# Graph-attention stack on one Trainium2 core: which operand is loaded and which is moved in the attention-times-values product of layers 0 and 1

## The chip, the core and the metric

The kernel runs on one core of one Trainium2 chip. The core has a matrix engine (PE, with its weight load shown apart as PEld), a vector engine (DVE), a scalar engine (ACT), a general engine (POOL, which here issues the gathers) and SyncE (SP, which issues the plain transfers); each takes its instructions in its own order and waits on semaphores of the others. The metric is the device time of one execution in microseconds (us). Three timed runs of the kernel before gave 2251.62, 2253.98 and 2256.02 us, median 2253.98 us.

## What is computed

Four graph-attention layers over 4096 nodes with 256 features, each followed by a residual sum and a layer norm. The adjacency matrix is 4096 x 4096 with about one entry in 256 set, and the diagonal. Layer 0, cut to what matters:

```
h = (x @ W.T)                       # 4 heads of 64
e[h,i,j] = leaky_relu(alpha_src[h,i] + alpha_dst[h,j], 0.2)
attn = softmax over j of e, only where adj[i,j] is set
out[i,h] = sum_j attn[h,i,j] * h[j,h]
x = layernorm(x + out)
```

Layer 1 has the same form with 4 heads of 64, layer 2 has 2 heads of 128, and layer 3 has one head of 256 with a positive and a negative attention, a product and an elu. The change touches the product attn x h of layers 0 and 1.

## The kernel before

**Tiling.** The 4096 nodes are 32 row tiles of 128 (`m`). A program at the start of the kernel (`lists`) finds, for each row tile, the nodes that any of its 128 rows has as a neighbour, and packs them into 13 groups of 128 nodes (`NG`), with the tile's own nodes as a fourteenth (`NP` = 14 positions). For a row tile the attention is then a sum over 14 blocks of 128 x 128 in place of 32. The 14 positions are worked in two halves of 7 (`HALF`).

**One row tile in layers 0 and 1.** `RowTile.load` fetches the scores of the 128 rows (`S`), the packed mask, and for each position 128 rows of values by an indirect gather that POOL issues (line 647; 13 of them, the fourteenth is a plain transfer). A gathered block `G[k]` holds, for each of 4 heads, 65 columns: 64 values already multiplied by the exponential of their score, and that exponential itself, whose weighted sum is the softmax's denominator (`C4` = 65). `RowTile.half` makes the weights `w[h]`, 128 neighbours x 128 rows for each position: heads 0 to 2 by ACT (line 712), head 3 by DVE (lines 704 and 708), and then a maximum and the mask by DVE for two heads at once (line 681: one instruction for heads 3 and 0, one for heads 1 and 2). Then the products: for head 3, 0, 1, 2 in turn and for each of the 7 positions, one fp32 matmul (line 724) in which the 65 value columns are loaded as the stationary operand and the 128 columns of weights move past them. The result, 65 x 128 for each head, is transposed to what is wanted; four heads side by side fill one PSUM bank of 512 columns (`accs[0]`), over both halves. `copy` (line 749, ACT) takes the 65 x 512 out of the bank into `aT`, `back` (line 757, PE) transposes it by heads into another bank, taken from `ptwo[1]`, as 128 x 260, and `finish` (lines 1114 to 1117, DVE) divides by the sums and adds the residual.

Each fp32 matmul shows in the trace as two pairs of a weight load and a matmul, so the 4 x 14 products of a row tile are 112 PE instructions and as many loads.

**Order.** `Layer.half_alone` writes the order of one half step: transposes of a row tile of the following layer, the half of tile m, then the store, the projection, the copy and back of tile m-1 (in part 0) or its finish (in part 1). So tile m-1's copy and back stand behind tile m's first half, and its finish behind the second. The bank `accs[0]` comes from a pool of two (`ptwo[0]`), so tile m+2 takes the bank of tile m. The order of instructions on each engine is laid out when the program is built, from this order, from what is ready and from estimated durations; the lists' work, the projections of the following layer and the attention are interleaved by it. Gathered blocks lie in 16 slots of two positions (`g0`), and from layer 1 on in 14 more (`g1`).

Layer 2 adds whole rows (`whole_rows`, lines 1016 to 1027): for three groups of four row tiles all 32 blocks are worked without packing, and these units fill in between the row tiles.

## Time and profile before

| | |
|---|---|
| median of three timed runs | 2253.98 us |
| span of the profiled execution | 2249.3 us |
| median less span | 4.7 us |
| mean granted PE clock | 0.966 of full speed |
| PE busy, share of the span | 2014.0 us, 90% |
| DVE busy | 1786.6 us, 79% |
| ACT busy | 1737.9 us, 77% |
| POOL busy | 1494.4 us, 66% |
| matmuls of line 724 (layers 0 and 1) | 7168, from 168.7 to 1339.1 us |
| copy of the accumulator, line 749 | 64, 0.57 us each |

The profiled execution's time outside its span isn't recorded on its own; its span is the time that the steps are summed against, and the runs' median lies 4.7 us above it. Read the table with care: busy shares are means over stages. The kernel passes through stages with different limits: building the lists with layer 0 (to about 646 us), the rest of layer 0 (to about 830), layer 1 (to about 1340), layer 2 with its whole rows (to about 1760) and layer 3. A group's idle column says how long the engine stood still before the group's instructions, and who released it; POOL's instructions have a fixed pause between them that is put down as "issue" or to whatever happened last.

### The profile page before, as it was taken

The numbers are of one execution on the slowest core, as the hardware profiler recorded it, in microseconds if no ns is written. First come the engines' busy times: TensorE is split into PE (matmuls) and PEld (weight loads), VectorE is DVE, ScalarE is ACT, GpSimd is POOL, SyncE is SP. The second block draws the span as 40 slices with busy tenths as digits, with TensorE's granted clock in tenths as the row PEclk, the third lists the DMA queues.
The fourth block names the chain that finished last, engine by engine and source line by source line (L and its number), as shares of the span: only waits on it lengthen the run. The fifth ranks groups of instructions, "written<-read, shape, count | busy, mean of one in ns | idle before, by whom it ended". The sixth has DMA issues, their size and how long they took to land. (4 is left out here: it accounts for less than half of the span.)

```text
span 2249.3 us, 49137 instructions
## 1 busy us (share of the span) xinstructions
PE 2014.0 (90%) x15689; PEld 1834.3 (82%) x15689; DVE 1786.6 (79%) x5060; ACT 1737.9 (77%) x4989; POOL 1494.4 (66%) x1597
## 2 busy tenths in 40 slices
PE   4878889989999969988899898989999999999995
PEld 2658788878899859988888798989998888788784
DVE  2889899999999959987988886887876566566566
ACT  4778988988789859987888776987876677667664
POOL 2107655656677777777777777777773477777773
PEclk7999999999999989999999999999999999999998
DMA  8879877777566665666665666777777688888884
GB/s 284 258 245 360 272 219 250 254 247 228 146 170 191 174 202 168 182 175 175 173 185 162 172 167 171 226 209 223 223 227 225 200 282 280 249 284 270 262 248 130
DMA packets 250319, 492.99 MB, mean 219 GB/s; under 512 B 44385, under 2 KB 156610, under 8 KB 249666
## 3 DMA queue, kind: packets, MB, share of 16 engines
q0 software_dynamic: 81536, 245.30, 38.3%
q1 hardware_dynamic: 163906, 240.26, 33.3%
q10 hardware_dynamic: 4608, 4.20, 0.5%
q8 instruction: 126, 2.06, 0.4%
q14 instruction: 143, 1.17, 0.2%
HBM read 437.05 MB, written 52.54 MB: 218 GB/s over the span
## 5 line engine op out<-in xcount | busy, mean ns | idle before, releaser
L647 POOL DMA_INDIRECT G<-vals,idx x1456 | 1480.7, 1017 | 715.7 <-issue 221.1
L712 ACT ACTIVATE w<-S,G 128x128 f32<-128x128 f32 x3248 | 1001.6, 390 | 140.6 <-DMA G<-vals,idx 101.6
L724 PE MATMUL bank<-w,G 128*65 128x128 f32 x7168 | 837.8, 276 | 59.7 <-DVE w L681 59.3
L724 PEld LDWEIGHTS bank<-w,G 128*65 128x65 f32 x7168 | 798.7, 140 | 69.9 <-DVE w L681 68.4
L681 DVE SCALAR_TENSOR_TENSOR w<-w,bank 128x1792 f32<-128x1792 f32 x256 | 514.6, 2013 | 13.4 <-ACT w L712 11.2
L727 PE MATMUL bank<-G,w 128*128 128x257 f32 (+1 forms) x2660 | 490.8, 342 | 25.7 <-ACT z L1102 13.6
L727 PEld LDWEIGHTS bank<-G,w 128*128 128x128 f32 x2660 | 431.9, 195 | 73.2 <-ACT z L1102 16.4
L1027 PE MATMUL bank<-vw,pw 128*128 128x129 f32 (+1 forms) x2048 | 298.5, 301 | 3.7 <-issue 2.3
L1027 PEld LDWEIGHTS bank<-vw,pw 128*128 128x128 f32 x2048 | 273.6, 191 | 20.1 <-issue 2.8
L690 ACT ACTIVATE w<-S,G 128x128 f32<-128x128 f32 x385 | 137.8, 393 | 136.8 <-DMA G<-vals,idx 90.0
L440 DVE TENSOR_SCALAR oh<-iota,place 128x256 bf16<-128x256 f16 (+2 forms) x992 | 221.8, 298 | 9.4 <-PE bank L446 9.1
L704 DVE TENSOR_TENSOR w<-S,G 128x256 f32<-128x256 f32 x384 | 151.9, 416 | 69.9 <-DMA G<-vals,idx 66.5
L446 PE MATMUL bank<-mk,oh 128*128 128x132 fp8e4 x2336 | 192.1, 226 | 13.8 <-ACT cm L453 7.0
L557 PE MATMUL bank<-wext,xT 128*128 128x268 f32 (+3 forms) x640 | 176.9, 409 | 16.9 <-ACT xT L548 14.1
L446 PEld LDWEIGHTS <-oh 128*128 128x128 bf16 x2336 | 146.9, 99 | 50.4 <-DVE oh L440 12.7
L385 ACT ACTIVATE mk<-raw 128x1024 uint8<-128x1024 int32 x128 | 130.5, 1051 | 28.0 <-DMA raw<-in_adjB_dram 27.7
L557 PEld LDWEIGHTS bank<-wext,xT 128*128 128x128 f32 x640 | 117.2, 200 | 36.0 <-ACT xT L548 16.9
L1017 DVE SCALAR_TENSOR_TENSOR pw<-pw,mw 128x512 f32<-128x512 f32 x192 | 127.6, 689 | 18.2 <-ACT pw L1016 17.5
L1016 ACT ACTIVATE pw<-Sw,d 128x512 f32<-128x512 f32 x192 | 133.2, 711 | 7.5 <-PE bank L1027 7.0
L714 DVE SCALAR_TENSOR_TENSOR w<-w,mk 128x896 f32<-128x896 f32 x80 | 86.6, 1086 | 41.1 <-ACT w L712 37.9
L1024 DVE TENSOR_TENSOR pw<-pw,mw 128x512 f32<-128x512 f32 x64 | 43.6, 691 | 85.4 <-ACT pw L1023 48.0
L692 DVE TENSOR_TENSOR w<-w,mk 128x896 f32<-128x896 f32 x55 | 60.0, 1091 | 59.5 <-ACT w L691 58.2
(140 smaller groups left out, 1563.3 us busy)
## 6 DMA issues: line engine op xcount, KB each, us to landing
raw<-in_adjB_dram SPq DMA_DIRECT2D x128, 512.0 KB
mk<-maskC SPq DMA_DIRECT2D x112, 231.0 KB
G<-vals,idx POOLq DMA_INDIRECT x1456
S<-edge SPq DMA_DIRECT2D x64, 256.0 KB
vw<-vals SPq DMA_DIRECT2D x96, 129.0 KB
xp<-y SPq DMA_DIRECT2D x96, 128.0 KB
y<-xp SPq DMA_DIRECT2D x96, 128.0 KB
mw<-maskW SPq DMA_DIRECT2D x20, 528.0 KB
```

Source lines behind the costliest of these rows:

```text
L440: nc.vector.tensor_scalar(oh[:, :n * P], iota[:, :n * P], self.place[:, it, j:j + 1], None, op0=ALU.is_equal)
L446: nc.tensor.matmul(accs[b][:, s * MC:(s + 1) * MC], oh[:, (k - a) * P:(k - a + 1) * P], mk[:, j, it, :].bitcast(FP8), start=touches[b][0] ...
L557: nc.tensor.matmul(pp[:, :c1 - c0], self.xT[:, k, :], wext[:, k, c0:c1], start=(k == 0), stop=(k == KT - 1 and brow is None))
L647: nc.gpsimd.indirect_dma_start(out=self.place(pos), out_offset=None, in_=sh["v"][n][:NODES[t], :], in_offset=bass.IndirectOffsetOnAxis(ap= ...
L681: nc.vector.scalar_tensor_tensor(pair, pair, LEAST, mh2, op0=ALU.max, op1=ALU.mult)
L690: nc.scalar.activation(w[0][:, k, :], S[:, 0, :], AF.Relu, bias=d(k, 0))
L704: nc.vector.tensor_tensor(w[h][:, k:k + 2, :], S[:, h:h + 1, :].to_broadcast([P, 2, P]), dd[:, :, V + T + h:V + T + h + 1].to_broadcast([P ...
L712: nc.scalar.activation(w[h][:, k, :], S[:, h, :], AF.Exp, bias=d(k, h))
L724: nc.tensor.matmul(accs[0][:Wd, h * P:(h + 1) * P], v, w[h][:, k, :], **how)
L727: nc.tensor.matmul(a, w[h][:, k, :], v, **how)
L1016: nc.scalar.activation(p, S[:, h], AF.Exp, bias=d)
L1027: nc.tensor.matmul(accs[it][:, c:c + Wd], p[:, it, :], v[:, c:c + Wd], start=(j == 0 and h == heads[0]), stop=(j == NT - 1), skip_group_ch ...
```

## The change

For heads 3 and 2 the roles are swapped: the weights (128 columns) are loaded and the 65 value columns move past them, so that the result is 128 rows x 65 columns, as wanted. Heads 0 and 1 stay as they were. The products of heads 3 and 0 alternate, position by position, then those of heads 2 and 1. The direct results stand in columns 256 to 385 of the bank, the transposed ones in columns 0 to 255. `copy` takes out 65 x 256 in place of 65 x 512, `back` transposes two heads in place of four, into columns 126 to 255 of the same bank, and `finish` reads columns 126 to 385 of it. No bank of `ptwo[1]` is taken for `back` any more, and `accs[0]` is held until `finish` has read it, where before it came free with `copy`. Layers 2 and 3 keep their products.

```diff
+TWOS = ((3, 0), (2, 1))
...
-            heads = list(range(A, H)) + list(range(A))
+            heads = range(H)
+        if n < 2:
+            for up, flat in TWOS:
+                for k in range(HALF):
+                    pos = half * HALF + k
+                    how = dict(stop=pos == NP - 1, skip_group_check=True)
+                    c = 2 * P + (up - 2) * Wd
+                    nc.tensor.matmul(accs[0][:, c:c + Wd], w[up][:, k, :], G[k][:, up * Wd:(up + 1) * Wd],
+                                     start=pos == 0 and up == TWOS[0][0], **how)
+                    nc.tensor.matmul(accs[0][:Wd, flat * P:(flat + 1) * P], G[k][:, flat * Wd:(flat + 1) * Wd],
+                                     w[flat][:, k, :], start=False, **how)
+            return
         for h in heads:
...
-                if n < 2:
-                    nc.tensor.matmul(accs[0][:Wd, h * P:(h + 1) * P], v, w[h][:, k, :], **how)
-                else:
-                    a = accs[h][:, :Wd] if n == 3 else accs[0][:, h * Wd:(h + 1) * Wd]
-                    nc.tensor.matmul(a, w[h][:, k, :], v, **how)
+                a = accs[h][:, :Wd] if n == 3 else accs[0][:, h * Wd:(h + 1) * Wd]
+                nc.tensor.matmul(a, w[h][:, k, :], v, **how)
...
-            self.aT = L.prog.ep.tile([C4, H4, P], F32, name="aT")
-            L.nc.scalar.copy(self.aT, self.accs[0][:C4, :].rearrange("p (h i) -> p h i", h=H4))
+            self.aT = L.prog.ep.tile([C4, 2, P], F32, name="aT")
+            L.nc.scalar.copy(self.aT, self.accs[0][:C4, :2 * P].rearrange("p (h i) -> p h i", h=2))
...
-        acc = L.prog.bank(L.prog.ptwo[1])
-        for h in range(H4):
-            L.nc.tensor.transpose(acc[:, h * C4:(h + 1) * C4], self.aT[:, h, :], L.shared["ident"][:C4, :C4])
-        self.accs = [acc]
+        for h in range(2):
+            c = 2 * P + (h - 2) * C4
+            L.nc.tensor.transpose(self.accs[0][:, c:c + C4], self.aT[:, h, :], L.shared["ident"][:C4, :C4])
+        self.accs = [self.accs[0][:, 2 * P - 2 * C4:2 * P + 2 * C4]]
```

## The prediction

> **What bounds the kernel now.** I read the busy time of each engine stage by stage first, since the change acts only where line 724 runs (169 to 1339 us). Columns: PE, PEld, DVE, ACT, POOL busy us (instructions), granted PE clock, DMA share, GB/s.

> ```profile
> 250.00:650.00 400.00, 363.53 (x3661) 331.54 (x3662) 394.45 (x1184) 346.32 (x1053) 249.45 (x245) 0.99 0.70 219
> 860.00:1300.00 440.00, 401.76 (x3391) 375.62 (x3390) 380.84 (x837) 376.52 (x1269) 334.51 (x347) 0.98 0.63 175
> 1300.00:1360.00 60.00, 59.39 (x488) 54.36 (x487) 47.02 (x142) 40.26 (x131) 45.27 (x45) 1.00 0.62 168
> 1360.00:1590.00 230.00, 210.84 (x1720) 204.44 (x1719) 176.96 (x431) 190.81 (x519) 180.30 (x164) 0.97 0.74 211
> 1590.00:1700.00 110.00, 110.00 (x913) 107.55 (x912) 89.78 (x242) 88.90 (x246) 81.07 (x72) 1.00 0.78 225
> ```

> While the lists are built (first row) DVE is busy 394.45 of 400 us: it is the bound, with 5.6 us to give. In layer 1 (second row) no engine looks full. There I read POOL's timeline (start, duration, idle before in brackets):

> ```profile
> 1001.08 0.94 POOL L647 DMA_INDIRECT G<-vals,idx  x1 [0.30 <-PE bank L724]
> 1002.33 0.95 POOL L647 DMA_INDIRECT G<-vals,idx  x1 [0.30 <-DVE u L1080]
> 1003.59 0.95 POOL L647 DMA_INDIRECT G<-vals,idx  x1 [0.30 <-PE bank L724]
> ...
> 1358.94 1.10 POOL L647 DMA_INDIRECT G<-vals,idx  x1 [1.61 <-DMA vals<-row]
> ```

> The pause of 0.30 us is the same whatever is named as releaser, so it belongs to the instruction. 347 gathers x 0.30 = 104 us, with 334.5 busy: 438.6 of 440 us. POOL is full. Followed through the whole trace, its gathers run without a longer pause from gather 302 at 646 us to 1685 us, but for one: the 1.61 us at 1358.94, where layer 2's first full gathers wait for the last rows that layer 1 stores. So from 646 to 1685 us a faster PE buys nothing except at that one place. From 1300 to 1360 and from 1590 to 1700 PE is full as well (59.39 of 60, 110 of 110): layer 1's tail and the end of layer 2 stand on PE.

> **The products.** The rows:

> ```profile
> L724 PE MATMUL bank<-w,G 128*65 128x128 f32 x7168 | 837.8, 276 | 59.7 <-DVE w L681 59.3
> L724 PEld LDWEIGHTS bank<-w,G 128*65 128x65 f32 x7168 | 798.7, 140 | 69.9 <-DVE w L681 68.4
> L681 DVE SCALAR_TENSOR_TENSOR w<-w,bank 128x1792 f32<-128x1792 f32 x256 | 514.6, 2013 | 13.4 <-ACT w L712 11.2
> ```

> Durations overlap, so I take starts. The PE and PEld timelines, merged runs:

> ```profile
> 1014.46 0.46 PE L757 MATMUL bank<-ident,aT 65*128 65x65 f32 x4
> 1014.76 3.22 PE L724 MATMUL bank<-w,G 128*65 128x128 f32 x28
> ...
> 211.81 1.42 PEld L278 LDWEIGHTS bank<-ablk,nat 128*128 128x128 f32 x12
> ```

> 28 matmuls of line 724 in 3.22 us, less the last one's 0.28, over 27 steps: 109 ns from start to start (128 columns moving). Each load starts 2 ns after the matmul before it, so one load hides behind one matmul and a step is the longer of matmul i and load i+1. What a load of 128 fp32 columns costs uncovered is seen in line 278, where only 4 columns move: (1.42 - 0.19)/11 = 112 ns a step. Scaled by columns (an estimate), a load of 65 is 57 ns and a matmul of 65 is 55 ns; the transposes of line 757, 65 columns moving behind loads of 128, step in 62 ns, which bounds the latter from above.

> One position of a pair of heads (3 and 0, or 2 and 1) is four PE instructions; before, 4 x 109 = 436 ns. After: the direct head's two matmuls of 65, the first covering a load of 128 (112), the second a load of 65 (57 to 62, I take 59); then the other head's two of 128, covering a load of 65 (109) and one of 128 (112). Sum 392 ns, 44 less. The two halves of an fp32 product are not interleaved by the change, so one load of 128 stays uncovered. 28 such pairs in a row tile: 1.23 us. Bounds: both direct steps held at 112 gives 442, a loss of 0.17 us a tile; loads hidden as far as their sum allows (2 x 112 + 2 x 57 = 338) a gain of 2.7 us.

> [...]

> **Back and copy.** Two transposes fewer: 2 x 62 = 0.12 us of PE a tile. ACT's copy (line 749, 0.57 us at 65 x 512) falls to 256 columns; the nearest row, a copy of 128 x 256 (line 548), takes 0.35: 0.22 us less, from nothing to 0.28. DVE, POOL and SP get the same instructions and transfers; finish reads as many columns.

> **The sum per engine.** PE 1.35 us x 64 = 86 us, ACT 14 us, of which almost all lies beside other work:

> - 646 to 1300 us: POOL hides it. Nothing. The cover goes only if gathers stop being the limit, which take 13 x 1.255 = 16.3 us a tile.
> - 163 to 646 us (22 tiles): DVE hides it. DVE's waits from 150 to 650 us that end on PE or ACT work: 5.6 us on line 446, 5.4 us on line 712. But 4.3 of the former stand behind ACT waiting 4.05 us for the adjacency's transfer, and the latter two follow ACT's waits of 2.5 and 3.6 us for the same. I take 2 us of the 11, ends 0 and 11.
> - Layer 1's tail: PE runs without a gap over 0.6 us from 1271 to 1364 us, some eight halves of 0.62 us saved and four tiles' transposes: up to 5.4 us. The masks of the last half are ready at 1329.8 and its matmuls start at 1333.1, so there is room for 3.3 us by its own data, somewhat more since its first pair's masks are ready 2 us sooner. POOL's 1.61 us goes with it; next late there are its own gathers. Layer 2 is bound partly by POOL (gain 1.6), partly by PE (up to 5.4): I take 3.

> Together 5 us: 2244.3 of span, and with the 4.7 us between span and median, **2249.0 us**.

> **Rivals.**
> 1. *PE's work counts more.* DVE's 11 us go wholly and PE carries its 5.4 into the end of layer 2, where it is full: -16, 2238 us. For: PE full at 1590 to 1700. Against: the transfer waits above, and PE's 6.5 us wait at 1364 for masks of line 714, which a PE that comes sooner only lengthens.
> 2. *The bank is held too long: slower.* `accs[0]` now comes free with finish (line 1115). In layer 1's steady part the first matmul of tile m+2 starts 0.1 to 2.3 us before that ends, in 19 of 30 tiles; there it must wait or DVE's order must turn. POOL's cover swallows it: counted by gathers, layer 1's tile 10 begins its gathers at 946.8 us in slots that tile 6 left at 927.0, 20 us earlier. In layer 0 the first matmul comes 2.7 to 5.5 us behind line 1115 while the lists run, so it doesn't bite, unless a new layout of the engines' orders puts finish more than 2.7 us later; then PE holds weights buffers, and the full DVE stands. Price: cycles of four tiles (copies at 261.1, 346.7, 434.4, 523.2, 607.0) took 83.9 to 88.8 us, mean 86.5; all at the worst, over 5.2 cycles, +12: 2266 us.
> 3. *It does nothing.* Loads of 128 hold both direct steps, or the tail is DVE's: 2254, within 2 us. The loss end is 0.17 us x 64 = 11 us of PE, also covered.

> **How the numbers follow.** The forecast (-2 to -8) 0.45, rival 1 0.20, rival 2 0.22, rival 3 0.13. 0.2%, about what a measurement can tell, is 4.5 us: of the forecast's chance 0.27 lies beyond it. Faster 0.27 + 0.20 = 0.47, same 0.18 + 0.13 = 0.31, slower 0.22. The range cuts off the far halves of rivals 1 and 2: 2240 to 2263. Faster and slower cases come partly from how the orders are laid out anew, which no row shows; the cycles' spread also works downwards (83.9: -14), inside rival 1.

> **What would show it.** Line 724's place taken by two forms, 128 and 65 columns, steps 112, 59, 109, 112; PE busy down some 40 us in layer 1 with POOL's 0.30 us pauses unchanged and the layer as long; gather 302 within 2 us of 646; the 1.61 us gone. Wrong if POOL shows longer pauses between 646 and 1340, if DVE falls below 97% while the lists run, or if PE's busy time does not fall.

## The result, and the profile after

The changed kernel takes 2267.96 us (median of 11 runs, 2257.16 to 2278.62); the kernel before, run beside it, takes 2253.06 us (11 runs, 2247.77 to 2257.99). The ratio is 1.0062, with a 95% interval of 1.0048 to 1.0077: **slower**, by some 14 us, where 2249.0 was forecast with a range up to 2263. The profiled execution of after took 2262.2 us, 5.8 less than its median (span 2260.5, mean granted clock 0.940 against 0.966 before).

Busy time by stage, after (columns as in the prediction: PE, PEld, DVE, ACT, POOL busy us, granted PE clock, DMA share, GB/s):

```profile
250.00:650.00 400.00, 354.35 (x3481) 323.27 (x3481) 381.73 (x1141) 329.67 (x1013) 235.74 (x238) 0.91 0.69 216
860.00:1300.00 440.00, 394.34 (x3441) 363.23 (x3441) 374.94 (x840) 379.49 (x1293) 334.56 (x347) 0.96 0.63 176
1300.00:1360.00 60.00, 54.77 (x447) 48.71 (x446) 50.61 (x152) 42.49 (x146) 45.82 (x47) 0.97 0.62 172
1360.00:1590.00 230.00, 205.41 (x1671) 199.69 (x1670) 171.50 (x406) 184.04 (x500) 180.51 (x163) 0.95 0.71 207
1590.00:1700.00 110.00, 107.94 (x884) 105.52 (x883) 92.29 (x254) 89.81 (x244) 83.00 (x76) 0.98 0.76 219
```

The first row is where the time went. DVE, which bounds the time in which the lists are built, fell from 394.45 to 381.73 us of 400, and the granted PE clock from 0.99 to 0.91. In the second row POOL is unchanged (334.51 before, 334.56 now, 347 gathers both times): layer 1 is as long as it was. PE's busy time fell there, as meant, but by 7.4 us and not by 40.

The place is dated by POOL's gathers, which all later work follows. The starts of the same gathers, after less before, from the traces: gather 13 -1.2 us, gather 100 +1.0, 200 +8.8, 302 +8.2, 310 +11.7, 410 +11.9, 832 +11.8, 859 +11.3, 1091 +9.0, 1455 (the last) +12.3. All of the loss is made between 170 and 660 us; layer 1 neither adds nor takes; some 3 us are won back from its tail to the end of layer 2, and lost again after that. These dates come from one execution each. That of after was 5.8 us faster than its median, and `old_products_early_mask` (below), at a ratio of 0.9993, strays from before by up to 4.2 us at these gathers, so differences of 3 us are read with care.

POOL's timeline, after (start, duration, idle before in brackets), in layer 1 and from gather 866, ahead of which the 1.61 us pause stood:

```profile
1001.01 0.95 POOL L649 DMA_INDIRECT G<-vals,idx  x1 [0.30 <-DVE mv L1068]
1002.26 0.95 POOL L649 DMA_INDIRECT G<-vals,idx  x1 [0.30 <-DVE b L1085]
...
1368.88 0.95 POOL L649 DMA_INDIRECT G<-vals,idx  x1 [0.30 <-issue]
1370.13 0.95 POOL L649 DMA_INDIRECT G<-vals,idx  x1 [0.30 <-issue]
```

The pauses of 0.30 us are the same as before, and the pause of 1.61 us is gone, as predicted: between gather 308 and gather 1094 POOL has one pause over 0.33 us left, 2.01 us ahead of gather 446 at 834.68, where before had 0.42 us at 826.43.

Now one tile while the lists are built. PE's timeline, before (line 724 the products, line 446 the matmuls that pack the mask of a later tile):

```profile
415.06 6.28 PE L724 MATMUL bank<-w,G 128*65 128x128 f32 x56
...
421.88 1.20 PE L446 MATMUL bank<-mk,oh 128*128 128x132 fp8e4 x18
423.34 0.43 PE L724 MATMUL bank<-w,G 128*65 128x128 f32 x2 [0.26 <-DVE w L681]
423.61 0.45 PE L446 MATMUL bank<-mk,oh 128*128 128x132 fp8e4 x5
423.90 0.38 PE L724 MATMUL bank<-w,G 128*65 128x128 f32 x2
424.12 1.78 PE L446 MATMUL bank<-mk,oh 128*128 128x132 fp8e4 x22
```

The same place after (line 726 the direct products, 728 the others, 448 the packing):

```profile
426.20 5.45 PE L448 MATMUL bank<-mk,oh 128*128 128x132 fp8e4 x72
433.35 0.44 PE L726 MATMUL bank<-G,w 128*128 128x65 f32 x2 [1.69 <-DVE w L683]
...
435.26 0.53 PE L726 MATMUL bank<-G,w 128*128 128x65 f32 x2
435.58 0.63 PE L728 MATMUL bank<-w,G 128*65 128x128 f32 x2
436.00 0.53 PE L726 MATMUL bank<-G,w 128*128 128x65 f32 x2
...
437.43 0.34 PE L726 MATMUL bank<-G,w 128*128 128x65 f32 x2
437.60 0.39 PE L728 MATMUL bank<-w,G 128*65 128x128 f32 x2
437.82 0.34 PE L726 MATMUL bank<-G,w 128*128 128x65 f32 x2
```

Three things are to be seen. **The steps**: from 437.43 to 437.82 one pair position takes 0.39 us, 0.17 of it the direct head's two matmuls and 0.22 the other's; 392 ns, 171 and 221 were predicted. **The order**: before, the packing is cut into pieces with attention matmuls between them; after, 72 packing matmuls stand in one block, 5.45 us long, and then PE stands for 1.69 us until the masks of line 683 are made. In the orders of PE's instructions, from the first attention matmul on, 31% of the packing matmuls are in unbroken blocks of 30 or more before (called long blocks below), 77% after. **The clock**: from 435.26 to 436.00 the same pair position takes 0.74 us. Four neighbouring stretches of 3.40 us of after, cut where the clock changes, say why (columns as above):

```profile
427.10:430.50 3.40, 3.40 (x51) 2.67 (x48) 3.40 (x17) 3.00 (x10) 2.79 (x3) 1.00 0.97 283
430.50:433.90 3.40, 1.68 (x18) 1.14 (x17) 3.40 (x8) 3.02 (x13) 2.48 (x4) 1.00 1.01 363
433.90:437.30 3.40, 3.40 (x21) 3.40 (x21) 3.19 (x10) 3.40 (x10) 0.49 (x1) 0.50 0.93 228
437.30:440.70 3.40, 3.40 (x36) 3.38 (x36) 3.40 (x8) 3.40 (x13) 1.28 (x2) 0.99 0.94 321
```

A stretch in which PE is busy for 1.68 of 3.40 us is followed by one at clock 0.50, with 21 matmuls in place of 36. The clock in the records of before and after is 1.0 or 0.5 and changes in steps of 3.41 us (but for the last of each trace, every record runs for a whole number of them). For each full-clock step I estimated how much of it PE spent moving columns, from the steps from start to start that these traces show at full clock (the packing's 132 columns mostly take 57 ns, so 0.43 ns a column; line 724's 128 f32 columns take 109, so 0.85 ns an f32 column): between 160 and 1340 us, 10 steps of before are followed by half clock, all with a share under 0.40, and 32 of after, 28 of them under 0.40 and the other four at 0.48 to 0.52; of the 581 steps of both that are not followed by it, 5 are under 0.40. Up to 0.52 the share doesn't decide it: 21 steps of after under 0.52 kept the full clock. Half clock between 163 and 646 us comes to 23.9 us before and 95.6 after.

An estimate of what it cost: 95.6 - 23.9 = 71.7 us more at half speed is up to 35.8 us of PE's work, and the shorter steps and the two transposes fewer save, at 1.35 us a tile, 1.35 x 22 = 29.7 us in that stage. By this estimate the clock can take back all that the matmuls had saved.

DVE's waits between 163 and 646 us (us in total, times, longest), before and then after:

```profile
DVE w L681 <- ACT w L712: 5.4, 2, 3.3
DVE oh L440 <- PE bank L446: 4.3, 1, 4.3
```

```profile
DVE oh L442 <- PE bank L448: 15.8, 17, 2.0
DVE w L683 <- ACT w L714: 4.0, 2, 2.2
```

The one-hots that DVE makes for the packing have 8 buffers (`oh`), so DVE can run 8 ahead of PE. DVE's timeline, before:

```profile
416.59 1.72 DVE L440 TENSOR_SCALAR oh<-iota,place 128x256 bf16<-128x256 f16 x8
...
419.93 1.42 DVE L704 TENSOR_TENSOR w<-S,G 128x256 f32<-128x256 f32 x4
421.27 2.01 DVE L681 SCALAR_TENSOR_TENSOR w<-w,bank 128x1792 f32<-128x1792 f32 x1
423.20 4.98 DVE L440 TENSOR_SCALAR oh<-iota,place 128x384 bf16<-128x384 f16 x22
```

and after:

```profile
420.89 0.98 DVE L442 TENSOR_SCALAR oh<-iota,place 128x256 bf16<-128x256 f16 x4
...
423.50 1.09 DVE L706 TENSOR_TENSOR w<-S,G 128x256 f32<-128x256 f32 x3
426.52 4.84 DVE L442 TENSOR_SCALAR oh<-iota,place 128x384 bf16<-128x384 f16 x22 [1.94 <-PE bank L448]
431.28 2.01 DVE L683 SCALAR_TENSOR_TENSOR w<-w,bank 128x1792 f32<-128x1792 f32 x1
```

Before, a mask of 2.01 us fills the time until PE has worked through the attention and frees the first one-hot; then come the other 22. After, the mask stands behind the 22, nothing is left for DVE to do, and the full engine waits 1.94 us. So two causes offer themselves: **C**, the clock (PE thinned out, its clock halved, DVE waiting for it), and **O**, the order (masks late, behind the one-hots), which would cost by itself. The bank that is held longer (rival 2) is a third.

### The profile page after: what moved, and what is told of

The parts are those of the page before. It is cut to its first block, busy times and chain, and to the rows that moved or that the text cites. A ratio compares the mean times of both kernels' runs of the same rounds, so it can differ in the third digit from the quotient of the medians.

```text
span 2260.5 us, 49097 instructions
## 1 busy us (share of the span) xinstructions
PE 1990.6 (88%) x15561; PEld 1807.3 (80%) x15561; DVE 1773.7 (78%) x5060; ACT 1725.5 (76%) x4989; POOL 1484.9 (66%) x1597
## 5 line engine op out<-in xcount | busy, mean ns | idle before, releaser
L726 PE MATMUL bank<-G,w 128*128 128x65 f32 x3584 | 647.4, 265 | 102.3 <-DVE w L683 89.3
L728 PE MATMUL bank<-w,G 128*65 128x128 f32 x3584 | 731.3, 288 | 0.0
L726 PEld LDWEIGHTS bank<-G,w 128*128 128x128 f32 x3584 | 587.3, 206 | 124.4 <-DVE w L683 102.5
L737 PEld LDWEIGHTS bank<-G,w 128*128 128x128 f32 x2660 | 430.2, 195 | 75.0 <-ACT z L1113 16.1
L728 PEld LDWEIGHTS bank<-w,G 128*65 128x65 f32 x3584 | 381.6, 149 | 0.3 <-issue 0.2
L559 PE MATMUL bank<-wext,xT 128*128 128x268 f32 (+3 forms) x640 | 184.3, 417 | 36.1 <-ACT xT L550 33.0
L448 PE MATMUL bank<-mk,oh 128*128 128x132 fp8e4 x2336 | 183.1, 226 | 8.6 <-DVE oh L442 4.8
```

Of the source, the lines that this page charges most:

```text
L448: nc.tensor.matmul(accs[b][:, s * MC:(s + 1) * MC], oh[:, (k - a) * P:(k - a + 1) * P], mk[:, j, it, :].bitcast(FP8), start=touches[b][0] ...
L559: nc.tensor.matmul(pp[:, :c1 - c0], self.xT[:, k, :], wext[:, k, c0:c1], start=(k == 0), stop=(k == KT - 1 and brow is None))
L726: nc.tensor.matmul(accs[0][:, c:c + Wd], w[up][:, k, :], G[k][:, up * Wd:(up + 1) * Wd], start=pos == 0 and up == TWOS[0][0], **how)
L728: nc.tensor.matmul(accs[0][:Wd, flat * P:(flat + 1) * P], G[k][:, flat * Wd:(flat + 1) * Wd], w[flat][:, k, :], start=False, **how)
L737: nc.tensor.matmul(a, w[h][:, k, :], v, **how)
```

## The experiments

The ratio is always to the kernel before on the same chip. On three of the chips every program, the kernel before too, took 22 to 24% longer, with pauses of PE and POOL that the trace puts down to "issue"; the twelve runs there (2757 us and more for the kernel before) are read only by their ratios to the kernel before there. The lists are bound otherwise there: between 163 and 810 us DVE waits 108.8 us for the packing in `own_bank`, where before has 4.3 in its whole list stage. So what a ratio there says of the other chips is not shown. The group of line 724 in `own_bank`, whose products are those of before (busy, mean ns, idle before, releaser), stood 59.7 us idle in before:

```profile
L724 PE MATMUL bank<-w,G 128*65 128x128 f32 x7168 | 959.4, 290 | 244.8 <-issue 211.4
```

| label | products | masks and packing | fillers | kernel before, us | ratio (95%) | half clock 163 to 646 us | gather 310, us late |
|---|---|---|---|---|---|---|---|
| (the change) | new | late | no | 2253 | 1.0062 (1.0048 to 1.0077) | 95.6 | 11.7 |
| new_products_early_mask | new | early | no | 2253 | 1.0046 (1.0029 to 1.0062) | 78.5 | 12.7 |
| old_products_late_mask | old | late | no | 2253 | 1.0104 (1.0080 to 1.0128) | 47.8 | 23.0 |
| old_products_early_mask | old | early | no | 2253 | 0.9993 (0.9976 to 1.0010) | 30.7 | 0.3 |
| new_products_filled_pack | new | late | all packs | 2253 | 1.0077 (1.0053 to 1.0102) | 41.0 | 14.0 |
| new_order_fill_3 | new | late | beside attention | 2254 | 1.0029 (1.0018 to 1.0040) | 34.1 | 3.7 |
| new_early_mask_fill_3 | new | early | beside attention | 2256 | 0.9984 (0.9973 to 0.9996) | 27.3 | -1.1 |
| layer0_only | new in layer 0 | late | no | 2789 | 1.0161 (1.0133 to 1.0189) | | |
| layer1_only | new in layer 1 | as before | no | 2789 | 1.0006 (0.9980 to 1.0032) | | |
| blocks_not_in_turn | new, heads in blocks | late | no | 2789 | 1.0381 (1.0354 to 1.0409) | | |
| own_bank | old | as before | no | 2789 | 0.9991 (0.9972 to 1.0011) | | |
| new_order_fill_beside | new | late | beside attention | 2791 | 1.0071 (1.0042 to 1.0100) | | |
| new_early_mask_fill_beside | new | early | beside attention | 2791 | 0.9947 (0.9926 to 0.9968) | | |
| old_products_fill_beside | old | not set; packing in long blocks | beside attention | 2791 | 1.0077 (1.0049 to 1.0106) | | |
| old_products_late_mask_fill_beside | old | late | beside attention | 2791 | 1.0153 (1.0116 to 1.0191) | | |
| new_order_fill_2 | new | late | beside attention | 2757 | 1.0059 (1.0029 to 1.0089) | | |
| new_early_mask_fill_2 | new | early | beside attention | 2757 | 0.9928 (0.9905 to 0.9951) | | |
| old_products_fill_2 | old | not set; packing in long blocks | beside attention | 2757 | 1.0052 (1.0030 to 1.0074) | | |
| layer1_only_2 | new in layer 1 | as before | no | 2757 | 0.9973 (0.9951 to 0.9995) | | |

"Late" is the order that the change brought with it, or one made like it; "early" the order of before, or one made like it. The labels say where the masks stand on DVE. Where the packing stands on PE came out of the laying out anew, fillers not counted, in long blocks: 77% in the change, 0% in `new_products_early_mask`, 96% in `old_products_late_mask`, 10% in `old_products_early_mask`, 91% in the changed products' late order with fillers beside attention, 76% in their early order with them, 86% in the old products with them and no order set. The two columns on the right are from the profiled execution, against the profile of before (23.9 us), and are left out on the chips with the pauses, where the granted clock is lower as well (0.890 over `own_bank`, 0.966 over before).

### Where, and the bank

`layer0_only` and `layer1_only` keep the products, copy and back of before in the other layer; the second has `DIRECT = (1,)`.

```diff
+DIRECT = (0,)
...
-        if n < 2:
+        if n in DIRECT:
```

> The change in layer 0 alone, layer 1 as before. Clock theory (A lighter PE leaves, once a row tile, a stretch in which only the pack's small matmuls run; in the trace of after 32 windows of 3.4 us between 160 and 1340 us have PE streaming for less than 0.52 of the time and each is followed by a halved clock, against 10 before; PE then falls behind and the full DVE waits for it): the whole loss is made in the list stage, so 2265 to 2270 us, gather 308 at 655 us or later (645.9 before, 657.6 after), half clock some 90 us between 163 and 646 us (24 before, 96 after). Order theory (the bank held until finish and the engines' orders laid out anew cost the DVE its waits; the clock only follows): the same 2265 to 2270.

> The change in layer 1 alone, layer 0 as before. Both theories: the list stage is as before (gather 308 at 646 us), layer 1 is held by POOL's gathers, its tail gives the 1.61 us pause of POOL and up to 2 us more of PE: 2249 to 2252 us. If the clock also costs in layer 1 and at its end (ten half-clock windows there after, three before; 13.6 us of half clock just after the boundary), 2253 to 2256.

Measured: 1.0161 and 1.0006. The loss comes with layer 0, on whose time the lists lie; by its gathers it is made before gather 302, which starts at 857.6 us in `layer0_only` and at 811.9 in `layer1_only`. In the order of PE's instructions 77% of the packing stands in long blocks in `layer0_only`, 31% in `layer1_only`. The products in layer 1 cost nothing clear of noise; a second run, `layer1_only_2`, gave 0.9973, so there may be a small gain in them.

> Layer 0 as before, the changed products in layer 1 alone; on the chip with pauses 1.0006. Theories C and O both put the whole loss into the time in which packs run beside layer 0, so layer 1 alone keeps that part as before: gather 310 within 2 us of the kernel before, and of the gain at layer 1's tail (the 1.61 us pause, up to 5.4 us of PE) what the end of layer 2 leaves: ratio 0.998 to 1.001. If the direct product costs by itself wherever it stands, 1.002 or more.

`own_bank` has the old products and takes only the bank's part of the change: `back` writes into the bank that it came from, which is so held until `finish` has read it.

```diff
-        acc = L.prog.bank(L.prog.ptwo[1])
+        acc = self.accs[0]
```

> The kernel before with one part of the change: the transposes of back go into the accumulators' own bank, which is so held until finish; products, copy and the four transposes as before. Clock theory: PE's work is that of before, 2251 to 2256 us. Order theory: the bank is what costs, 2260 to 2268.

Measured: 0.9991 (0.9972 to 1.0011), on a chip with the pauses. Holding the bank costs nothing clear of noise with the old products, and the order of the packing stays as before (31% in long blocks). Rival 2's mechanism falls, as far as that chip can tell.

`blocks_not_in_turn` works each head's seven positions in a row, so that the direct products of a head stand together.

```diff
             for up, flat in TWOS:
                 for k in range(HALF):
                     pos = half * HALF + k
                     how = dict(stop=pos == NP - 1, skip_group_check=True)
...
                     nc.tensor.matmul(accs[0][:, c:c + Wd], w[up][:, k, :], ...
+                for k in range(HALF):
+                    pos = half * HALF + k
+                    how = dict(stop=pos == NP - 1, skip_group_check=True)
                     nc.tensor.matmul(accs[0][:Wd, flat * P:(flat + 1) * P], ...
```

> All of the change but the turns: within a pair of heads first the 7 direct products, then the 7 others, so that every load of 128 columns stands behind a direct matmul. By the steps of after (112, 59, 109) a pair's half takes 14 x 109 + 13 x 112 + 59 = 3041 ns, as before (28 x 109 = 3052). Bank, copy, back and finish as in the change. Clock theory: PE is as loaded as before, half clock between 163 and 646 us falls from 96 us towards the 24 of before, time 2251 to 2256. Order theory: the bank is held as long as in the change, 2262 to 2268.

Measured: 1.0381, the slowest of all, where both theories had foreseen no more than the change's loss. It ran only where PE has the pauses as well, so its size isn't carried over, and why it is so slow there stays open.

### Order and products apart

The edit ties the first mask of a tile's second half to the last 22 one-hots of a pack: the mask first ("early"), or behind the last one-hot ("late"). Only the order is set; no work is added. The diff is the early form; the late one makes the mask depend on the last one-hot.

```diff
+    def order(self, mask):
+        for oh in self.ohs[-22:]:
+            self.tc.add_manual_dep(oh.ins, mask.ins.name, mybir.DependencyInfo(
+                mybir.DependencyClass.NoSync, mybir.DependencyReason.DATA), reason="order")
...
+                    mask = masked(pairs[h // 2])
+                    if n == 0 and half == 1 and h == 0:
+                        prog.order(mask)
```

> The whole change, and one order added on DVE while the lists are built: the last 22 of a tile's 31 one-hots (line 440 before) are issued behind the first mask of the tile's second half (line 681). The kernel before was laid out so in 15 places of that stage; the change, and the kernel with the products not in turn, have 24 to 30 one-hots there and both masks after them, so that PE has 72 of the pack's small matmuls in one run with no attention between. Order theory, in this form: the loss goes, ratio to before 0.994 to 1.000, half clock in the list stage no more than before. Clock theory in its first form (a lighter PE leaves quiet stretches whatever the order): ratio stays 1.004 to 1.010.

> The kernel before, products and all, with one order added on DVE: the first mask of a tile's second half is issued behind the last of the one-hots that the tile's pack makes. Order theory: the change's loss without the change, ratio 1.004 to 1.015, half clock in the list stage three times before's or more. Clock theory in its first form: PE is as loaded as before, ratio 0.998 to 1.002.

> The kernel before with the early order of the first run of this call in every tile; it tells what the order is worth by itself. Order theory: 0.996 to 1.000, since before has it in most tiles. Clock theory in its first form: 1.000.

Measured: 1.0046, 1.0104 and 0.9993. The late order, with the products of before, costs by itself more than the whole change, though it is a stricter late order than the change's (96% of the packing in long blocks against 77%): PE's timeline of `old_products_late_mask` shows the pattern of after, with line 734 the old products and 454 the packing.

```profile
429.19 1.20 PE L454 MATMUL bank<-mk,oh 128*128 128x132 fp8e4 x18
430.88 4.70 PE L454 MATMUL bank<-mk,oh 128*128 128x132 fp8e4 x54 [0.49 <-DVE oh L448]
437.27 6.33 PE L734 MATMUL bank<-w,G 128*65 128x128 f32 x56 [1.69 <-DVE w L689]
```

So O is a cause. But the early order gave the new products back only a part (1.0062 to 1.0046, with intervals that overlap), and gather 310 was no earlier (12.7 us late against 11.7, in an execution that was 0.6 us over its median where that of after was 5.8 under). DVE's wait for the packing fell from 15.8 to 3.7 us; other waits for PE took its place. This is `new_products_early_mask` (line 1135 reads what `back` left, line 778):

```profile
DVE w L691 <- ACT w L722: 7.1, 6, 4.1
DVE rec L1135 <- PE bank L778: 6.5, 3, 2.3
DVE oh L450 <- PE bank L456: 3.7, 7, 1.2
```

Of DVE's 28.5 us of idle time between 163 and 646 us in that run, 25.6 lie in a half-clock stretch or in the 6.8 us behind one, by the trace; such time makes up 42% of the stage. In the change itself it is 14.5 of 27.6 us, with 45% of the stage, so there the trace doesn't tie DVE's waits to the clock.

The four kernels without fillers can be read in pairs. Exchanging the products adds 48 us of half clock under either order (30.7 to 78.5, 47.8 to 95.6), and the late order 17 us with either product. With the early order the exchange costs 0.53% (0.9993 to 1.0046): the order alone doesn't explain the change, and C is left for the rest. With the late order the new products are the faster ones (1.0104 to 1.0062), but these two late orders are not the same.

### The clock kept up

To keep the clock up without taking anything from the products, the packing gets further matmuls by a block of zeros (`none`), 30 to a pack by the trace. They add nothing to the sums.

```diff
+        none = cst.tile([P, P], BF16, name="none")
+        nc.vector.memset(none, 0.0)
...
+                        if k == a and touches[b][0] != (j, k):
+                            nc.tensor.matmul(accs[b][:, s * MC:(s + 1) * MC], none, mk[:, j, it, :].bitcast(FP8),
+                                             start=False, stop=False, skip_group_check=True)
```

> The change in its own (late) order, with one more matmul of zero weights for each one-hot of the pack, which adds nothing to the result and keeps PE streaming: about 29 of 0.057 us in a tile, 1.7 us. If the halved clock is how the late order costs time: ratio 0.997 to 1.003 and the half clock in the list stage well under the change's. If the clock is a bystander and DVE simply waits for PE's order: 1.006 to 1.012, PE being 1.7 us a tile slower.

Measured: 1.0077, which looks like a no. The gathers say otherwise: gather 13 is already 12.2 us late, because the packs of the first ten tiles, which run ahead of any attention, got fillers too; from there to gather 310 only 1.8 us more are lost, where the change loses 12.9. Half clock fell from 95.6 to 41.0 us. So the fillers were next left out of those packs:

```diff
-                        if k == a and touches[b][0] != (j, k):
+                        if m >= LEAD and k == a and touches[b][0] != (j, k):
```

These four, with the change's own order, the early order, and both orders of the old products, ran where PE has the pauses:

> The changed kernel with its own order, and in each pack of row tiles 10 to 31 (those packed beside the attention) about 26 further matmuls by a block of zeros, which add nothing to the sums; the packs of tiles 0 to 9 have none, so the 12 us that the fillers cost ahead of 163 us in the earlier run with them must be gone. Theory C (thin 3.4 us windows of PE halve its clock, and DVE then waits for PE): half clock between 163 and 646 us falls from 95.6 us to under 50, gather 310 comes within 3 us of the kernel before, ratio 0.997 to 1.003. Theory O (PE stands for the masks because a pack of 72 lies in front of them, whatever its clock): the fillers make the block longer, gather 310 stays 11 us or more late, ratio 1.006 to 1.012.

> The changed products, the mask ahead of the last 22 one-hots as in the kernel before, and the same fillers in the packs of row tiles 10 to 31. Theory C: without fillers this order gave 1.0046 with 78.5 us of half clock between 163 and 646 us; with them under 45 us, gather 310 within 2 us of the kernel before, ratio 0.996 to 1.001. If what the early order left open is not the clock but the products themselves (their loads), the fillers add 1.5 us a tile to PE and the ratio stays at 1.004 to 1.008.

> Control: the kernel before with the same fillers in the packs of row tiles 10 to 31. Its half clock between 163 and 646 us is 23.9 us already, so there is little to win. Theory C: ratio 0.998 to 1.002, half clock under 25 us. If the fillers help by something else than the clock (by spreading the pack, say), they help here too: ratio below 0.996. If their 1.5 us of PE a tile costs by itself: 1.004 or more.

> The kernel before with its masks held behind all one-hots of the pack (which alone gave 1.0104, with 47.8 us of half clock between 163 and 646 us), and the same fillers. Theory C alone: half clock falls under 25 us and the ratio to 1.000 to 1.004. Theory O (the order costs by itself): the ratio stays at 1.009 to 1.013, whatever the clock does.

Measured: 1.0071, 0.9947, 1.0077 and 1.0153. The fillers don't help the old products; they cost them time. They also moved their packing into long blocks (86%, against 31%), so this control doesn't hold the order still. The late order stays slower than the early one by 1.0071/0.9947, so by 1.2%. Three of them were run again, and this chip had the pauses too:

> The changed kernel with its own order and fillers (matmuls by a block of zeros, about 26 to a pack) in the packs of row tiles 10 to 31, as in the earlier run on the chip with pauses, here for the comparison without them. Theory C (thin 3.4 us windows of PE halve its clock, and DVE waits for PE): half clock between 163 and 646 us falls from 95.6 us to under 50, gather 310 comes within 3 us of the kernel before, ratio 0.997 to 1.003. Theory O (the late masks cost by themselves): gather 310 at least 8 us late, ratio 1.005 to 1.012. If the chip again shows PE pauses put down to issue, only the ratio to the kernel before on that chip is read: 1.007 as measured there.

> The changed products, masks ahead of the last 22 one-hots, and fillers in the packs of row tiles 10 to 31. Without the fillers 1.0046, with 78.5 us of half clock between 163 and 646 us. Theory C: under 45 us of half clock, gather 310 within 2 us of the kernel before, ratio 0.995 to 1.000. If the products themselves hold PE (their uncovered loads), the 1.5 us a tile of fillers are added: ratio 1.004 to 1.008.

> Control: the kernel before with the same fillers. Half clock between 163 and 646 us is 23.9 us without them, so theory C sees little to win: 0.998 to 1.002. If the fillers help in a way that has nothing to do with the clock, below 0.996 here too; if their PE time costs, 1.004 or more (on the chip with pauses it was 1.0077).

Measured: 1.0059, 0.9928 and 1.0052, the same picture. At last the two with the new products ran on chips without the pauses:

> The changed products, masks ahead of the last 22 one-hots, fillers in the packs of row tiles 10 to 31; 0.9947 and 0.9928 on the chip with pauses on PE. On a chip without them, theory C: under 45 us of half clock between 163 and 646 us (78.5 without the fillers), gather 310 within 2 us of the kernel before, ratio 0.995 to 1.001. If the products themselves hold PE, the fillers add 1.5 us a tile to it: ratio 1.004 to 1.008, gather 310 at least 12 us late. If the chip has the pauses again: 0.990 to 0.996.

> The changed kernel with its own order (late masks) and the fillers in the packs of row tiles 10 to 31; 1.0071 and 1.0059 on the chip with pauses on PE. On a chip without them, theory C (the halved clock is the whole loss): under 50 us of half clock between 163 and 646 us, gather 310 within 3 us of the kernel before, ratio 0.997 to 1.003, as the early order with fillers (0.9984). Theory O (the late order costs by itself, beside the clock): gather 310 at least 6 us late, ratio 1.004 to 1.010.

Measured: 0.9984 (0.9973 to 0.9996) and 1.0029 (1.0018 to 1.0040). The stage of the lists, first in `new_early_mask_fill_3`, then in `new_order_fill_3`:

```profile
250.00:650.00 400.00, 355.67 (x4206) 343.30 (x4205) 396.83 (x1189) 339.77 (x1049) 242.96 (x244) 0.99 0.71 221
```

```profile
250.00:650.00 400.00, 351.68 (x4085) 337.65 (x4085) 387.81 (x1158) 331.11 (x1020) 242.01 (x237) 0.98 0.70 217
```

Of the two expectations, the early one came out as C had it (27.3 us, gather 310 within 2 us, a ratio in its range), and not as the rival that the new products hold PE by their loads (1.004 to 1.008). The late one fell between: its ratio lies in C's range, its gather 310, 3.7 us late, in neither's.

With both mended, DVE is busy 396.83 of 400 us, more than in the kernel before (394.45), the clock is 0.99, and gather 310 comes 1.1 us ahead of before. With the clock kept up but the order late, DVE is at 387.81, and its wait for the packing is nearly what it was. DVE's waits, again in this order:

```profile
DVE oh L452 <- PE bank L461: 1.0, 1, 1.0
```

```profile
DVE oh L444 <- PE bank L453: 12.4, 16, 1.7
```

So on the new products the fillers are worth 0.33% under the late order (1.0062 to 1.0029) and 0.62% under the early one (1.0046 to 0.9984), and the early order 0.16% without the fillers and 0.45% with them. The 0.16% is not clear of noise, the other three are. O is shown by the last pair, which have nearly the same half clock (27.3 and 34.1 us) and differ by 0.45%, and by the old products (0.9993 against 1.0104). It lies in the mask's place, not in the block: `new_early_mask_fill_3` has 76% of its packing in long blocks and is the fastest. C is shown less cleanly. The exchange of products under the early order and the fillers both point to it, but the fillers also laid PE's packing out anew (from 0% to 76% in long blocks under the early order), and no run changes the clock alone. That each hides a part of the other's gain is what the four ratios suggest. `new_early_mask_fill_3` is faster than the kernel before, by 0.04 to 0.27%.

What stays open: the fillers without the pauses were not run on the old products, so that they do nothing there but cost rests on the other chips (1.0077 and 1.0052) and on another order. Nor was it tried why the order was laid out anew; that it came with the change's edits to layer 0 is shown (`layer0_only` 77%, `layer1_only` and `own_bank` 31%), and that the estimated durations of the shorter matmuls moved it is only argued.

## Why the prediction was wrong, by its own steps

- **The products' steps: right.** 112, 59, 109 and 112 ns were predicted, and the starts in the trace of after step by 59, 112, 112 and 109 at full clock (medians, from the direct head's first matmul on), the same 171 for the direct head and 221 for the other, and 392 in sum. That loads run beside matmuls is shown: of a position's four loads three mostly start 1 to 3 ns after the start of the matmul ahead of them and one 55 ns after. Which step is the long one isn't as the prediction had it: the 59 ns stand ahead of a matmul with a load of 128, so "the longer of matmul i and load i+1" gave the sum and not each step.
- **PE busy down some 40 us in layer 1: wrong in size**, 7.4 us. One term left out is the clock: half clock there went from 13.7 to 34.7 us, which makes the same matmuls longer, by at most 10.5 us. That is a third of what is missing; the window after also holds 50 more PE instructions (3441 against 3391), and the rest is open. It cost nothing there.
- **ACT's copy, 0.22 us less: right.** 0.57 us fell to 0.356 (median of line 759), 0.21 less.
- **646 to 1300 us, POOL hides it: right.** POOL's busy time is unchanged, its pauses too but for the 2.01 us at 834.68, and gathers 310 to 859 stay between 11.1 and 13.6 us behind before. The gather that the prediction puts at 646 us is number 308 by the trace, not 302, which starts at 634.5; after comes 11.7 us late at the one and 8.2 at the other, so the sign "within 2 us of 646" failed on either reading.
- **163 to 646 us, "DVE hides it ... I take 2 us of the 11, ends 0 and 11": the step that failed.** It measured some -13 us (gather 13 to 310). The step took DVE's waits for PE as something that a faster PE can only shrink, so that the worst end was nothing. The traces showed in its place full-clock steps of PE with less moving in them (mean share between 163 and 646 us 0.82 before and 0.71 after, by the estimate above), 71.7 us more of half clock, and an order laid out anew that moved the mask which had filled DVE's wait (DVE's wait for the packing went from 4.3 to 15.8 us). The prediction's own sign was there to see: it called itself wrong if DVE fell below 97% while the lists run, and DVE is at 95.4%.
- **Layer 1's tail, 3 us: POOL's 1.6 shown, the rest not.** The 1.61 us pause is gone, and between gathers 859 and 880 all five profiles with the new products from chips without the pauses win 1.3 to 1.7 us, the two with the old products 0.1 and 0.4. From gather 832 to 1091 after wins 2.8 us, but the old products win 3.4 and 4.5 there too (`old_products_early_mask`, `old_products_late_mask`), so a gain of PE beyond the pause isn't shown. By the last gather after has lost 3.3 us again; why is open.
- **Rival 2, the bank: its price was near by luck, its mechanism wrong.** +12 us was its worst; `own_bank` shows no cost. Its clause on "a new layout of the engines' orders" pointed to the right thing, but the layout bit by DVE's mask and not by `finish`. Rivals 1 and 3 fell with the failed step.
- **The clock** was read in the first view (0.99 and 0.98) and then used for nothing. No row was asked what it would be with less on PE.
- The forecast, 2249.0 us, is 0.9978 of the shown median. With both causes mended the kernel stands at 0.9984. That the two are near is no confirmation: that kernel also has fillers and a mask order set by hand, and the forecast's own terms account for 1.6 us of shown gain. What was worked out was the change under unchanged order and clock.

## What to carry to other kernels

Before making a matmul shorter on an engine that is not the bound, look in the trace at how full the steps are in which its clock is granted (3.41 us here) and what follows the thin ones: in this kernel 38 of the 42 drops to half clock between 160 and 1340 us, before and after together, came behind a step with an estimated share under 0.40, so that the work taken away may be paid back at half clock, and an engine that waits for it may pay too. A control that adds instructions can change the order as well, so count the order in the control's own trace. Where orders are laid out from durations, a changed duration is a changed order: look in the profile for work that now fills a full engine's wait (here a 2 us mask between 8 and 22 one-hots), count what it costs if it is moved, and set that order by hand. When a control shows a loss, date it by a steady series of events (here the gathers), as a cost ahead of the stage can hide that the stage itself was mended.
